# Layer norm statistics on another engine, a later place for a finished half's last pieces in a Mamba scan, and expert products one block ahead

## The chip, the cores and the metric

The kernel runs on one core of a Trainium2 chip. The time is the device time in microseconds of one execution of the whole program, and the time of a kernel is the median over its runs. A core has five engines with a queue of instructions each: TensorE (PE in the profile; its weight loads are shown as PEld), VectorE (DVE), ScalarE (ACT), GpSimd (POOL) and SyncE (SP), which issues DMAs. The engines run beside each other and wait for each other with semaphores; each takes its own instructions in order. What lies in SBUF or in PSUM (TensorE's output memory, 8 banks) has up to 128 partitions, and a tile of "128x512" has 128 partitions of 512 numbers.

## The reference, cut to what matters

The input x has the shape 4 x 1024 x 128: 4 sequences of 1024 tokens, 128 features each, so 4096 tokens. Two blocks are computed one after the other, each with two feed-forward layers around an attention-like layer, with a layer norm ahead of every layer and the layer's result added to x:

```python
x = x + 0.5 * moe(layernorm(x))        # a
x = x + mamba(layernorm(x))
x = x + 0.5 * moe(layernorm(x))        # b, the same weights
x = x + 0.5 * soft(layernorm(x))       # a: soft mixture of experts
x = x + gla(layernorm(x))              # gated linear attention
x = x + 0.5 * soft(layernorm(x))       # b, the same weights

def layernorm(x):                # over the 128 features, no weights
    return (x - mean(x)) / sqrt(var(x) + 1e-5)
```

The three kinds of layer that the change touches, shortened:

```python
def moe(x):       # 8 experts, each token goes to its best 2, limited room
    gates, idx = top_k(softmax(x @ wg), 2); gates /= gates.sum()
    disp = rows of x brought together by expert          # 8 x cap x 128
    h = relu(disp @ w1[e] + b1[e])                       # 512 wide
    out = h @ w2[e] + b2[e]
    return sum over k of gates[k] * valid[k] * out[idx[k], loc[k]]

def mamba(x):     # inner width 256, 16 states
    u, z = split(x @ W_in); u = silu(conv4(u) + conv_b)
    dt, B, C = split(u @ W_xproj); delta = softplus(dt @ W_dt + b_dt)
    h[t] = exp(delta[t] * A) * h[t-1] + delta[t] * B[t] * u[t]   # 256 x 16
    y[t] = sum over states of h[t] * C[t];  y += u * D
    return (y * silu(z)) @ W_out

def gla(x):       # 16 heads of 8
    q, k = silu(x @ Wq), silu(x @ Wk);  v = x @ Wv
    f, g = sigmoid(x @ Wf1 @ Wf2), sigmoid(x @ Wg1 @ Wg2)
    S[t] = f[t] * S[t-1] + k[t] v[t];  o[t] = q[t] . S[t] / sqrt(8)   # S: 8 x 8 per head
    og = o * g;  og = og / sqrt(mean over a head of og^2 + 1e-5)
    return (og * norm_weight) @ Wo
```

The variance of a layer norm is that of the 128 features of one token, mean of squares of the differences from the mean.

## The kernel before

x stays in SBUF as 32 tiles of 128 tokens (NT = 32, each 128 tokens x 128 features), for the whole kernel. Most of the stages are written in a `with tc.manual_schedule(engines=ENGINES)` block, in which the order of the instructions on PE, DVE, ACT and POOL is the order of the Python lines; SP's DMAs are placed by a scheduler. So "ahead of" in the following means ahead in an engine's queue, and an instruction that waits holds up all that stand behind it on its engine.

**Layer norm.** `ln_stats` (L118) takes four tiles: per tile a bn_stats (L121) and a bn_aggr (L122) on DVE give mean and variance, and one add of eps (L123) follows for the four. `ln_root` (L127) takes the power of -1/2 on POOL (L130) and makes -mean * rstd, called nmr, on DVE (L133). `ln_apply` (L141) then normalises a tile in one ACT instruction, with rstd as scale and nmr as bias (L143). The statistics of a layer's norm are taken by the layer before it, when it has added its result to four tiles of x. Behind Mamba and behind gated attention, `ln_root` runs for 16 tiles at a time (around L1560 to L1590), elsewhere for 4.

**Experts** (`moe_layer`, L148). The tokens' normalised rows lie in DRAM; a block of 512 rows of one expert is fetched by four indirect DMAs that POOL issues (`gather`, L346), turned by PE (`turn`, L364, copied by DVE at L366), multiplied by w1 (`hidden`, L374, relu on ACT at L378), multiplied by w2 (`output`, L388) and written back to DRAM by four indirect DMAs of POOL (`scatter`, L352). There are 16 blocks and 64 gathers and 64 scatters per layer. The loop runs, per block, hidden of this block, gathers of the block three ahead (`AHEAD = 3`) between scatters of the block before, turn of the next block, and output of this one. Where no gather is left a `memset` of one column, called spacer, stands in its place (L412). Then the results are read back, weighted (L427 on ACT) and added to x.

**Mamba** (`mamba_layer`, L441). Each sequence is cut into two halves of 512 tokens: 8 halves. A half has 16 steps, one per state n, for all 512 tokens and 256 inner features (NC = 2 groups of 128). Of each state: `fetch` brings B and C to all partitions (DMAs on SP, or for some states a PE product, L610), `feed` makes dBu = du * B (L616 to L620, on POOL for ten states of sixteen, on DVE for six), `decay` makes exp(delta * A) on ACT (L628, twice), `scan` runs the recurrence on DVE (L638, twice), `keep` saves the last state for the next half (L649, ACT), `times_c` multiplies by C on POOL (L654), and `sums` adds up over the states on PE (L663 for the direct term, L669). A half's `prologue` (L484: transposes, convolution, projections, softplus as Ln and Exp at L577, and du and its like on DVE at L579 to L583) is issued in pieces between the steps of the half before it. A half's `epilogue` (L673) is a generator of pieces: zs = zs * py on DVE (L676), the product with W_out on PE (L682), the addition to x on DVE (L688) and the statistics. In the loop over k (state n of half i, k = 16 i + n) the epilogue of a finished half starts at the step with n = 2, and one piece of it is issued per step, ahead of the rest of the step.

**Gated attention** (`gla_layer`, L1318). Also in 8 halves of 512 tokens, with a loop over scan steps k of NU per half; per step PE spreads v over the partitions (L1433), DVE multiplies by k (L1439) and scans (L1450), POOL multiplies by q (L1458), PE sums (L1472). The prologue of the next half (xT copied by ACT at L1402, products on PE at L1407 to L1414, two silus on ACT at L1408, the copy of v at L1412, the thin product at L1416, the gates at L1424) and the epilogue of the one before are issued in pieces between. The epilogue: og on DVE (L1481), its square on ACT (sq, L1485), sums per head on PE (pm, L1489), root and reciprocal (L1494, L1496), spread back (pr, L1499), og again (L1503), the product with Wo on PE (L1506), the addition to x (L1510) and the statistics.

Of the kernel before, what the change touches and what calls it, by code (L numbers as in the profile page):

```python
# [8 lines left out]
F32 = mybir.dt.float32  # L9
# [59 lines left out]
def macaron_kernel(ctx: ExitStack, tc: tile.TileContext, a: dict, out: bass.AP):  # L69
# [67 lines left out]
    def ln_group(ln, j0):  # L137
        ln_stats(ln, j0)
        ln_root(ln, j0)

    def ln_apply(dst, j, ln):  # L141
        _, rstd, nmr = ln
# [5 lines left out]
    def moe_layer(w1, w2, b2, tag, ln, after):  # L148

        xn_d = dram.tile([T, D], F32, name=f"xn_d{tag}")  # L150
        with ExitStack() as s:
# [180 lines left out]


            with ExitStack() as s1:
                gp = s1.enter_context(tc.tile_pool(name=f"gath{tag}", bufs=16))
                wk = s1.enter_context(tc.tile_pool(name=f"ework{tag}", bufs=2))
                yp = s1.enter_context(tc.tile_pool(name=f"ey{tag}", bufs=3))
                ps = s1.enter_context(tc.tile_pool(name=f"eps{tag}", bufs=2, space=PSUM))
                psh = s1.enter_context(tc.tile_pool(name=f"epsh{tag}", bufs=3, space=PSUM))
                NBLK = NSB // 4  # L340
                gs, dTs, hTs, eos = {}, {}, {}, {}
                spacer = wk.tile([P, 1], F32, name="spacer")
# [53 lines left out]

                AHEAD = 3
                with tc.manual_schedule(engines=ENGINES):  # L400
                    for c in range(AHEAD * 4):
                        gather(c)
                    turn(0)
                    for blk in range(NBLK + 1):
                        if blk < NBLK:
                            hidden(blk)
                        for i in range(4):
                            c = (blk + AHEAD) * 4 + i
                            if c < NSB:
                                gather(c)  # L410
                            elif blk > 0:
                                nc.gpsimd.memset(spacer, 0.0)  # L412
                            if blk > 0:
                                scatter((blk - 1) * 4 + i)
                        if blk + 1 < NBLK:
                            turn(blk + 1)
                        if blk < NBLK:
                            output(blk)

# [21 lines left out]
    def mamba_layer(ln, ln_next):  # L441
# [3 lines left out]
        with ExitStack() as s:  # L445
# [227 lines left out]
            def epilogue(r):  # L673

                zs = r["zs"]
                nc.vector.tensor_tensor(zs, zs, r["py"], ALU.mult)  # L676
                yield
                yield
                po = ps.tile([P, NJ, D], F32, name="po", tag="mm")
                for i in range(NJ):  # L680
                    for c in range(NC):
                        nc.tensor.matmul(  # L682
                            po[:, i, :], zs[:, c, i * P : (i + 1) * P], w_out[:, c, :],
                            start=(c == 0), stop=(c == NC - 1),
                        )
                yield
                jj = r["b"] * (S // P) + r["h"] * NJ
                nc.vector.tensor_tensor(  # L688
                    x[:, jj : jj + NJ, :], x[:, jj : jj + NJ, :], po, ALU.add
                )  # L690
                yield
                ln_stats(ln_next, jj, NJ)
                yield


# [8 lines left out]
            with tc.manual_schedule(engines=ENGINES):  # L704

                for _ in prologue(*halves[0], rs[0], psa, "dA"):
                    pass
                for k in range(3):
                    at(fetch, k)
                at(feed, 0)  # L710
                at(feed, 1)
                at(decay, 0)
                at(decay, 1)
                LEAD = 5
                ahead, old, behind = (iter(()) for _ in range(3))
                for k in range(-LEAD, len(units) + 7):
                    if k % DS == DS - LEAD and (k + LEAD) // DS + 1 < len(rs):
                        i = (k + LEAD) // DS + 1
                        old, ahead = ahead, prologue(*halves[i], rs[i])
                    if k < 0:  # L720
                        next(ahead, None)
                        continue
                    if k > DS and k % DS == 2:
                        behind = epilogue(rs[k // DS - 1])
                    next(behind, None)
                    at(fetch, k + 3)
                    at(scan, k)
                    at(keep, k)
                    at(decay, k + 2)
                    at(times_c, k - 1)  # L730
                    at(feed, k + 2)
                    at(sums, k - 2)
                    next(old, None)
                    next(ahead, None)
# [583 lines left out]
    def gla_layer(ln, ln_next):  # L1318
        with ExitStack() as s:
# [158 lines left out]
            def epilogue(u):  # L1478
                r = rs[u]
                og = wk.tile([P, HB], F32, name="og")  # L1480
                nc.vector.scalar_tensor_tensor(  # L1481
                    og, r["po"], HD ** -0.5, r["fg"][:, 1, :], ALU.mult, ALU.mult
                )
                sq = wk.tile([P, HB], F32, name="sq")
                nc.scalar.activation(sq, og, AF.Square)  # L1485

                pm = ps.tile([P, P], F32, name="pm", tag="mm")
                for i in range(4):
                    nc.tensor.matmul(  # L1489
                        pm[i * 32 : (i + 1) * 32, :], hsel, sq[:, i * P : (i + 1) * P],  # L1490
                        start=True, stop=True,
                    )
                rn = wk.tile([P, P], F32, name="rn")
                nc.scalar.activation(rn, pm, AF.Sqrt, bias=eps_t, scale=1.0 / HD)  # L1494
                yield
                nc.vector.reciprocal(rn, rn)  # L1496
                pr = ps.tile([P, HB], F32, name="pr", tag="mm")
                for i in range(4):
                    nc.tensor.matmul(  # L1499
                        pr[:, i * P : (i + 1) * P], hback[:, i, :], rn, start=True, stop=True  # L1500
                    )
                yield
                nc.vector.scalar_tensor_tensor(og, og, nw, pr, ALU.mult, ALU.mult)  # L1503
                py = ps.tile([P, NJ, D], F32, name="py", tag="mm")
                for i in range(NJ):
                    nc.tensor.matmul(  # L1506
                        py[:, i, :], og[:, i * P : (i + 1) * P], wo, start=True, stop=True
                    )
                yield
                nc.vector.tensor_tensor(  # L1510
                    x[:, u * NJ : (u + 1) * NJ, :], x[:, u * NJ : (u + 1) * NJ, :], py, ALU.add
                )
                ln_stats(ln_next, u * NJ)
                yield


# [46 lines left out]
    spool2 = ctx.enter_context(tc.tile_pool(name="softw2", bufs=1, side="right"))  # L1563
    ew, eb = expert_weights(spool2)
    for j in range(0, NT, 16):
        ln_root(lns[2], j, 16)
    moe("b", lns[2], lambda j: ln_group(lns[3], j))

    def rest(soft):
        soft("a", lns[3], lambda j: ln_group(lns[4], j))  # L1570
        gla_layer(lns[4], lns[5])
        for j in range(0, NT, 16):
            ln_root(lns[5], j, 16)
        soft("b", lns[5], last=True)

    bounded = nc.values_load(flag, min_val=0, max_val=1)
# [87 lines left out]
```

## Time and profile before

| quantity | value |
|---|---|
| median of 9 runs | 2324.6 us |
| lowest and highest of them | 2322.81 and 2333.39 us |
| profiled execution, its own time | 2333.12 us |
| its span, first to last instruction | 2331.3 us |
| mean granted clock of TensorE in it | 0.911 |
| PE busy | 1926.1 us (83%) |
| DVE busy | 1412.7 us (61%) |
| POOL busy | 1397.4 us (60%) |
| ACT busy | 929.1 us (40%) |

By stage, from the timeline of the profiled execution: experts a with their routing to about 276 us, Mamba 276 to 860, experts b to about 1140, soft a 1140 to 1640, gated attention 1640 to 1830, soft b 1830 to 2331. The granted clock is the share of full speed at which TensorE was let run.

How to read the profile's lines. In the list of groups a line has the source line, engine, operation, output and inputs, their shapes and the count; then busy us in all and mean ns of one; then the engine's idle time just before these instructions, and what ended most of it ("<-DVE hst L638" is: DVE's work on hst at line 638). In the timeline a line has start, duration (of the whole run of like instructions, "x6" being six), engine, source line, operation, tiles, and in brackets the idle time before and its releaser. "issue" is time in which an engine waited for nothing that the profile shows.

### The profile page before, as it was taken

To read this page: it belongs to the slowest core of one execution; us is meant where nothing else is said; L and a number is where in the kernel's file an instruction comes from. 1 tells how busy PE (TensorE), PEld (TensorE's weight loads), DVE (VectorE), ACT (ScalarE), POOL (GpSimd) and SP (SyncE) were. 2 spreads that over 40 slices of the span, in tenths; PEclk is the share of its full clock that TensorE was granted. 3 is DMA by queue.
4 is the path that set the end of the run, shared out by engine and by line. 5 is a ranking of instruction groups with operands and counts; after the bars stand their busy time and mean duration, and the time that the engine had idled before them with its cause. 6 is when DMAs were issued, how large, how long until landed. Compare 5 with 4: busy or idle time off the path is not lost. (4 is left out here: it accounts for less than half of the span.)

```text
span 2331.3 us, 17972 instructions
## 1 busy us (share of the span) xinstructions
PE 1926.1 (83%) x5889; PEld 902.5 (39%) x5889; DVE 1412.7 (61%) x1947; ACT 929.1 (40%) x1453; POOL 1397.4 (60%) x896
## 2 busy tenths in 40 slices
PE   4788267889888855875499989999889799989998
PEld 3565122333333224654144434444223344434443
DVE  4311548898888965111777764556787677754444
ACT  3232265666555523322333333332553333333331
POOL 2677248888888961776355556664444455556663
PEclk9999679989999985898699999999897799999999
DMA  6111332323223233112100000000000000000000
GB/s 244 37 51 51 97 114 92 114 92 115 96 92 113 102 134 94 51 53 78 38 0 1 1 1 1 1 0 0 6 1 0 1 0 0 1 1 5 10 10 15
DMA packets 63677, 111.23 MB, mean 48 GB/s; under 512 B 7999, under 2 KB 41423, under 8 KB 58581
## 3 DMA queue, kind: packets, MB, share of 16 engines
q1 hardware_dynamic: 45062, 81.37, 10.5%
q0 software_dynamic: 8192, 16.79, 2.3%
q10 hardware_dynamic: 10322, 11.85, 1.5%
q8 instruction: 48, 0.79, 0.1%
q14 instruction: 53, 0.43, 0.1%
HBM read 90.53 MB, written 19.44 MB: 47 GB/s over the span
## 5 line engine op out<-in xcount | busy, mean ns | idle before, releaser
L891 POOL TENSOR_TENSOR dm<-ex,sm 128x1024 f32<-128x1024 f32 x128 | 244.6, 1911 | 218.2 <-DVE sm L887 125.3
L654 POOL TENSOR_TENSOR hc<-hst,Cs 128x1024 f32<-128x1024 f32 x128 | 287.9, 2260 | 78.2 <-DVE hst L638 74.8
L669 PE MATMUL py<-hc,ident 128*128 128x512 f32 x512 | 280.3, 679 | 44.2 <-POOL hc L654 44.0
L999 POOL TENSOR_TENSOR acc<-acc,L 128x1024 f32<-128x1024 f32 x96 | 225.9, 2353 | 117.1 <-ACT L L991 116.4
L991 ACT ACTIVATE L<-pl,pbc 128x512 f32<-128x512 f32 x256 | 162.1, 684 | 284.3 <-PE pl L981 279.9
L870 PE MATMUL l<-phiT,xT 128*128 128x512 f32 x512 | 245.8, 604 | 15.4 <-ACT xT L861 8.7
L879 ACT ACTIVATE ex<-l,nmh 128x1024 f32<-128x1024 f32 x128 | 142.7, 1115 | 285.2 <-DVE nmh L874 283.1
L981 PE MATMUL pl<-xT,phiM 128*128 128x512 f32 x512 | 245.2, 604 | 0.0
L1025 PE MATMUL py<-L,yt 128*128 128x512 f32 x512 | 238.4, 593 | 4.4 <-DVE L L1015 4.4
L902 PE MATMUL px<-dm,xn 128*128 128x512 f32 x512 | 240.8, 593 | 0.9 <-POOL dm L891 0.9
L874 DVE TENSOR_REDUCE nmh<-l 128x1 f32<-128x1024 f32 x128 | 156.6, 1223 | 107.5 <-PE l L870 107.5
L628 ACT ACTIVATE dA<-delta,A 128x512 f32<-128x512 f32 x256 | 179.3, 722 | 94.2 <-DVE hst L638 91.3
L620 POOL TENSOR_TENSOR dBu<-du,Bs 128x1024 f32<-128x1024 f32 x80 | 172.8, 2160 | 39.5 <-ACT dA L628 39.5
L669 PEld LDWEIGHTS py<-hc,ident 128*128 128x128 f32 x512 | 98.2, 206 | 209.1 <-issue 122.4
L378 ACT ACTIVATE hT<-ph,cols 128x512 f32<-128x512 f32 x128 | 88.0, 687 | 219.6 <-PE ph L374 216.4
L638 DVE TENSOR_TENSOR_SCAN hst<-dA,carry,dBu 128x512 f32<-128x512 f32 x128 | 154.2, 1260 | 5.6 <-POOL dBu L620 5.6
L886 DVE TENSOR_REDUCE sm<-ex 128x32 f32<-128x1024 f32 x128 | 154.8, 1209 | 0.0
L870 PEld LDWEIGHTS l<-phiT,xT 128*128 128x128 f32 x512 | 97.1, 193 | 145.8 <-issue 115.1
L638 DVE TENSOR_TENSOR_SCAN hst<-dA,dBu 128x512 f32<-128x512 f32 x128 | 146.6, 1200 | 7.6 <-POOL dBu L620 7.5
L352 POOL DMA_INDIRECT y_d<-eo,dest x128 | 125.9, 983 | 35.7 <-issue 24.1
L1015 DVE TENSOR_TENSOR L<-L,rd 128x1024 f32<-128x1024 f32 x128 | 147.0, 1212 | 0.1
L1025 PEld LDWEIGHTS py<-L,yt 128*128 128x128 f32 x512 | 96.8, 190 | 127.3 <-issue 117.0
(248 smaller groups left out, 2897.3 us busy)
## 6 DMA issues: line engine op xcount, KB each, us to landing
Cs<-bc_d SPq DMA_DIRECT2D x32, 1024.0 KB, 4.6
Bs<-bc_d SPq DMA_DIRECT2D x80, 256.0 KB, 3.1
w<-in_w SPq DMA_DIRECT2D x4, 2048.0 KB
y<-y_d SPq DMA_DIRECT2D x32, 256.0 KB, 3.5
y_d<-zero SPq DMA_DIRECT2D x1, 4096.0 KB
ew<-in_ew ACTq DMA_DIRECT2D x1, 4096.0 KB
x<-in_x SPq DMA_DIRECT2D x8, 256.0 KB, 7.9
xn_da<-xn ACTq DMA_DIRECT2D x8, 256.0 KB, 14.4
```

The source lines that it names most:

```text
L620: eng.tensor_tensor(dBu, r["du"], r.pop(("B", n)).unsqueeze(2).to_broadcast([P, HB, NC]), ALU.mult,)
L628: nc.scalar.activation(dA, r["delta"][:, :, c], AF.Exp, scale=A[:, c * DS + n : c * DS + n + 1],)
L638: nc.vector.tensor_tensor_scan(hst[:, :, c], r.pop(("dA", n, c)), dBu[:, :, c], 0.0 if h == 0 else carry[b][:, c, n : n + 1], ALU.mult, AL ...
L654: nc.gpsimd.tensor_tensor(hc, r.pop(("h", n)), Cs.unsqueeze(2).to_broadcast([P, HB, NC]), ALU.mult)
L669: nc.tensor.matmul(r["py"][:, c, :], ident, hc[:, :, c], start=False, stop=(n == DS - 1))
L870: nc.tensor.matmul(l[:, q * 512 : (q + 1) * 512], xT[:, j * P : (j + 1) * P], phiN[:, o : o + 512], start=True, stop=True,)
L891: nc.gpsimd.tensor_tensor(dms[k], exs.pop(k), sms.pop(k).unsqueeze(2).to_broadcast([P, NG, PS]), ALU.mult,)
L902: nc.tensor.matmul(px[hf * 2 + q], xns[j // 4][:, j % 4, :], dmf[:, q * 512 : (q + 1) * 512], start=(j == 0), stop=(j == NT - 1),)
L981: nc.tensor.matmul(pl[:, i, :], phiM[:, (2 * c + i) * P : (2 * c + i + 1) * P], xT[:, t * TB : (t + 1) * TB], start=True, stop=True,)
L991: nc.scalar.activation(L[:, i, :], pl[:, i, :], AF.Exp, bias=pbc[:, 2 * c + i : 2 * c + i + 1], scale=-1.0,)
L999: nc.gpsimd.tensor_tensor(accs[t], accs[t], L, ALU.add)
L1025: nc.tensor.matmul(pys[t], yt[:, 2 * c + i, :], L[:, i, :], start=(c + i == 0), stop=(c == CS - 1 and i == 1),)
```

## The change: two sets of statistics on ScalarE, a reordered step, one more block in flight

There are three parts.

1. In the experts' loop the transposes run two blocks ahead and the first product one block ahead of the second; gathers are issued four blocks ahead. Buffers grow with it: 20 gathered tiles instead of 16, 3 work buffers instead of 2, 4 PSUM buffers of the first product instead of 3.
2. In Mamba's loop the piece of a finished half's epilogue is issued after `fetch` and `scan` of the step and no longer ahead of them.
3. The statistics behind Mamba and behind gated attention are taken by a new function on ACT: four Copies with their sums accumulated, one small instruction that makes -mean, four Squares of x - mean with their sums accumulated, one small instruction that makes var + eps. They use the same three tiles per layer norm. The root follows in a new function with both its instructions on POOL.

```diff
+    def ln_stats_act(ln, j0, n=4):
+        mv, rstd, nmr = ln
+        js = slice(j0, j0 + n)
+        junk = small.tile([P, D], F32, name="junk")
+        for j in range(j0, j0 + n):
+            nc.scalar.activation(junk, x[:, j, :], AF.Copy, accum_out=mv[:, j, 0:1])
+        nc.scalar.activation(nmr[:, js], mv[:, js, 0], AF.Copy, scale=-1.0 / D)
+        for j in range(j0, j0 + n):
+            nc.scalar.activation(
+                junk, x[:, j, :], AF.Square, bias=nmr[:, j : j + 1], accum_out=mv[:, j, 1:2]
+            )
+        nc.scalar.activation(
+            rstd[:, js], mv[:, js, 1], AF.Identity, bias=eps_t, scale=1.0 / D
+        )
+
+    def ln_root_pool(ln, j0, n=4):
+        _, rstd, nmr = ln
+        js = slice(j0, j0 + n)
+        nc.gpsimd.tensor_tensor(
+            rstd[:, js], rstd[:, js], half_t.to_broadcast([P, n]), ALU.pow
+        )
+        nc.gpsimd.tensor_tensor(nmr[:, js], nmr[:, js], rstd[:, js], ALU.mult)
...
-                gp = s1.enter_context(tc.tile_pool(name=f"gath{tag}", bufs=16))
-                wk = s1.enter_context(tc.tile_pool(name=f"ework{tag}", bufs=2))
+                gp = s1.enter_context(tc.tile_pool(name=f"gath{tag}", bufs=20))
+                wk = s1.enter_context(tc.tile_pool(name=f"ework{tag}", bufs=3))
...
-                psh = s1.enter_context(tc.tile_pool(name=f"epsh{tag}", bufs=3, space=PSUM))
+                psh = s1.enter_context(tc.tile_pool(name=f"epsh{tag}", bufs=4, space=PSUM))
...
-                AHEAD = 3
+                AHEAD = 4
                 with tc.manual_schedule(engines=ENGINES):
                     for c in range(AHEAD * 4):
                         gather(c)
                     turn(0)
+                    turn(1)
+                    hidden(0)
                     for blk in range(NBLK + 1):
-                        if blk < NBLK:
-                            hidden(blk)
+                        if blk + 2 < NBLK:
+                            turn(blk + 2)
+                        if blk + 1 < NBLK:
+                            hidden(blk + 1)
                         for i in range(4):
...
-                        if blk + 1 < NBLK:
-                            turn(blk + 1)
                         if blk < NBLK:
                             output(blk)
...
-                ln_stats(ln_next, jj, NJ)
+                ln_stats_act(ln_next, jj, NJ)
...
-                    next(behind, None)
                     at(fetch, k + 3)
                     at(scan, k)
+                    next(behind, None)
                     at(keep, k)
...
-                ln_stats(ln_next, u * NJ)
+                ln_stats_act(ln_next, u * NJ)
...
     for j in range(0, NT, 16):
-        ln_root(lns[2], j, 16)
+        ln_root_pool(lns[2], j, 16)
...
         for j in range(0, NT, 16):
-            ln_root(lns[5], j, 16)
+            ln_root_pool(lns[5], j, 16)
```

## The prediction

> **What bounds the kernel now.** I read first the shares, then the costliest groups by shape, then the timeline of each stage that the diff touches, because no engine bounds the whole span. TensorE (PE) is busy 83% of it, but the two soft stages (1140 to 1640 and 1830 to 2331 us), where it is the bound, are not touched. Of the touched rows the groups say:
>
> ```profile
> L654 POOL TENSOR_TENSOR hc<-hst,Cs 128x1024 f32<-128x1024 f32 x128 | 287.9, 2260 | 78.2 <-DVE hst L638 74.8
> L352 POOL DMA_INDIRECT y_d<-eo,dest x128 | 125.9, 983 | 35.7 <-issue 24.1 <-DMA y_d<-eo,dest 6.1 <-DVE dT L366 5.2
> L121 DVE BATCH_NORM_STATS2 st<-x 128x6 f32<-128x128 f32 x192 | 51.8, 280 | 7.9 <-DMA x<-in_x 7.4
> L143 ACT ACTIVATE xn<-x,nmr,rstd 128x128 f32<-128x128 f32 x192 | 83.2, 483 | 25.0 <-issue 15.4 <-DVE nmr L133 7.4 <-DMA xn_da<-xn 2.2
> L427 ACT ACTIVATE y<-y,gate 128x128 f32<-128x128 f32 x64 | 20.3, 389 | 42.5 <-DMA y<-y_d 26.6 <-DVE y L431 11.8 <-DVE x L435 2.8
> L676 DVE TENSOR_TENSOR zs<-zs,py 128x1024 f32<-128x1024 f32 x8 | 9.8, 1221 | 40.8 <-PE py L669 40.8
> L649 ACT COPY carry<-hst 128x2 f32<-128x2 f32 x64 | 12.2, 190 | 88.1 <-DVE hst L638 87.6
> ```
>
> In **Mamba** (276 to 860 us, halves about 67.6 us apart by the starts of zs, 399.27 and 466.89) POOL, DVE and PE are nearly level at 57 to 59 us of work per half, so a wait passes from one to the next. At a half's end zs holds up DVE, and all scans behind it, until the last sum is done. Here it is, DVE and then POOL:
>
> ```profile
> 399.27 1.22 DVE L676 TENSOR_TENSOR zs<-zs,py 128x1024 f32<-128x1024 f32 x1 [4.91 <-PE py L669]
> 400.41 7.15 DVE L638 TENSOR_TENSOR_SCAN hst<-dA,carry,dBu 128x512 f32<-128x512 f32 x6
> ```
> ```profile
> 403.03 2.14 POOL L654 TENSOR_TENSOR hc<-hst,Cs 128x1024 f32<-128x1024 f32 x1 [3.00 <-DVE hst L638]
> ...
> 418.19 2.13 POOL L654 TENSOR_TENSOR hc<-hst,Cs 128x1024 f32<-128x1024 f32 x1 [2.56 <-DVE hst L638]
> ```
>
> The first POOL wait (3.00) comes from zs, the second (2.56) from the statistics, which held DVE from 413.16 to 415.66 ahead of two scans.
>
> In the **experts** POOL's indirect DMAs are the bound: one every 1.28 us from 75.4 to 239.2 us (0.97 to 0.99 busy, 0.30 between), 128 of them, with no larger hole, while PE waits for each block's gathers:
>
> ```profile
> 208.43 0.33 PE L364 MATMUL pt<-ident,g 128*128 128x128 f32 x1 [2.28 <-DMA g<-xn_da,src]
> ```
>
> In **gated attention** (1640 to 1830) the clock of PE decides, as the table by windows shows; its columns are busy time of PE, weight loads, DVE, ACT, POOL, then the granted clock:
>
> ```profile
> 1680.00:1700.00 20.00, 17.37 (x78) 5.77 (x76) 18.88 (x27) 10.91 (x18) 9.72 (x5) 1.00 0.00 0
> 1740.00:1760.00 20.00, 18.64 (x59) 6.58 (x56) 14.80 (x22) 6.92 (x13) 9.45 (x4) 0.74 0.00 1
> ```
>
> At full clock DVE sets a half's time (18.88 of 20): 19.4 us from og to og. From 1720 on, a half takes 23.8 us, and the bound is a loop: sq on ACT, PE's output products, xT, PE's next projections, the v copy, sq. In it ACT waits for PE, and PE for ACT:
>
> ```profile
> 1715.14 0.59 ACT L1412 COPY qkv<-pq 128x512 f32<-128x512 f32 x1 [1.74 <-PE pq L1411]
> 1716.12 0.58 ACT L1416 COPY lr<-p 40x512 f32<-40x512 f32 x1 [0.40 <-PE p L1414]
> ```
> ```profile
> 1738.41 0.43 PE L1489 MATMUL pm<-sq,hsel 128*32 128x128 f32 x8 [1.27 <-ACT sq L1485]
> ```
>
> **The new statistics, S per four tiles.** Off DVE go 4 bn_stats, 4 bn_aggr and the add: 2.4 us in place. On ACT come 10 instructions, each behind the one before; no row of the trace has an accumulating one. From below: four Copies with a scale as the L427 row (0.389) and four Squares with a bias the same, plus two of 0.19 (the smallest row, L649): 3.5. From above: eight of 0.483 (L143, two pointers) and an extra 0.19 each for reading the accumulator out, and the two small ones: 5.8. A Square resembles L143 less than L427, but every sum must leave the engine, so I take 0.389 + 0.19 for each of eight, and 0.38: S = 5.0. Copy, Square and Identity bring no table load: the compiled kernels have 85 each.
>
> The Trainium skill, "ScalarE: Activation LUTs", Rules for kernel authors, says that such elementwise work belongs on VectorE and not on ScalarE. The rows agree as far as they go (2.4 us against 3.5 to 5.8), and by the rule alone both moves would lose; whether they do is decided by which engine has slack.
>
> **Mamba.** Two things leave DVE's path. fetch and scan now stand ahead of zs, so one scan (2.4 us) runs in the 4.91 us wait; fetch has PE's pb product or SP's Bs and Cs reads in it, and these only come sooner; the epilogue issues no DMA. zs stays where it was, since PE ends the last sum at 399.24. Retimed by hand, the product of state 2 starts 3.0 us sooner; that of state 6 is then held by PE's sums (three hc buffers, the third sum ends at 414.9), so 3.1 of the 5.56 is left. Against it: on ACT the statistics stand behind the silu block (408.34 to 411.6) and two decays, ahead of the decay of state 8, the copy of dbc and the next half's softplus. With S = 5.0 the scan of state 8 gains 2.2 us at most; the softplus, for which DVE then waits (three waits on ACT l, 29.3 us, of which one at the stage's start is 28.2), 1.2 to 2.5. I take 2.0 for each of six boundaries, and the whole 2.6 for the seventh, where the statistics are the only stall (822.57): 6 x 2.0 + 2.6 = **-14.6**. Bounds: all zs and statistics stalls at the seven (42.6 in sum) gone from below; 1.0 a boundary, -8, from above. The cover is ACT's 44 us of work in 67.6; without it S stands on the path, +2.6 a half.
>
> **Roots on POOL.** nmr moves behind pow for four 128x16 groups: it saves a 0.475 row of DVE and adds at most the pow's 2.9 on POOL. One of the two in gated attention stands amid waits of 1.3 to 5.1 us there; the others lie in the tails, and are in what follows.
>
> **Experts.** The 128 DMAs on POOL and their order by kind stay, four spacers of 0.12 come in, so 164 us stay. Twenty gathers instead of sixteen go ahead of the first scatter, at 101.7, when PE's first block ends at 101 to 102: 0 to 0.8 late. At the end POOL has five blocks of pure scatters (5.1 us each from 213.3), PE takes 8.4 us a block, and block 14 is ready at 228.6 as its slot comes: 0 to 3 late. I take **+1.3** for both layers (0 to +4); nothing can be gained while POOL's pitch holds.
>
> **Gated attention.** The 2.4 us leave DVE, which is the bound only at full clock. On ACT they stand between silu and the v copy, whose waits (1.74 and 0.40) swallow a part; sq comes 5.0 - 2.14 = 2.9 later once, and then each half's loop is longer. At a clock as in 1740 to 1760: 23.9 + 2.9 = 26.8. At full clock the loop is ACT's 10.4, S, and waits of 0.42, 4.39 and about 0.6: 20.8, against 19.4. Behind sq, PE's pm waits, with the spread and sums of the next states behind it, and DVE's scans behind those. PE's gap there grows from 1.3 to between 2.6 and 3.5 us.
>
> What that does to the clock is the largest unknown. Gaps of 1.27 to 1.40 us in this stage were followed by half clock in four of six halves; gaps of 2.5 to 3 in Mamba (423 to 426, 446 to 453) were; those of 2.2 in the experts (granted 0.97 there) mostly not. I take the first half at full clock, as its gap of 1.4 was harmless before, and the rest at half: intervals 19.5, 20.9, 23.9, 23.8 become 20.8, 26.8, 26.8, 26.8, which is +1.3 +5.9 +2.9 +3.0, with the first delay 2.9: **+16.0**. All at full clock: 2.9 + 1.3 - 0.1 - 3.1 - 3.0 = -2.0. All at half: +22.0.
>
> The page "TensorE: Matmul & The Clock Gate" of the Trainium skill (Part 1) has the clock halve only after an idle window of about 3.4 us. The 1.27 us gap above, with half clock from 1740.7, speaks against that being all; by the page the stage would mostly keep its clock, an estimate of -2 for the loop.
>
> Later than the loop: the last two halves have no projections, ACT has 10 to 17 us free before sq, but sq of the last stands behind the statistics of the one before, and soft b's first xT copy behind three of the last four Squares: **+2.5** (2 to 3).
>
> **Sum.** -14.6 + 1.3 + 16.0 + 2.5 = +5.2. The profiled execution took 2333.1 (span 2331.3 and 1.8 around), 8.5 above the median of nine, 2324.6; the difference is put on the median: 2338.3 on the profile's scale, **2329.8** on the median's.
>
> **Rivals.**
> *Clock kept (faster).* PE never loses its clock in gated attention, since the new gap (2.6 at full clock) is nearer to the experts' harmless 2.2. The point from which it decides: at most one of the four intervals at half clock. Loop -2.0, Mamba at 2.2 a boundary -15.8, others +3.8: -14.0, 2310.6. Against it: 1.3 us sufficed before.
> *ACT is next late in Mamba.* The statistics hold back the decays; 1.0 a boundary and 2.6: -8.6, and +11.2 in all, 2335.8. For it: DVE already waits on ACT for l. Against: ACT's 88.1 us of idle time at L649.
> *Half clock in every half of gated attention.* +22.0 in place of +16.0: 2335.8.
> *The experts turn PE-bound at their ends:* +4 in place of +1.3, 2332.5.
> *POOL's stalls in Mamba vanish as a whole,* -30 with some PE pitch left: +16.0 + 2.5 + 1.3 - 30 = -10, 2314.4. Against: hc buffers wait for PE's sums.
>
> **How the numbers follow.** Forecast 0.30 (own range 2325 to 2336), clock kept 0.25, ACT late 0.20, every half 0.14, experts 0.04, stalls gone 0.07. The measurement can tell about 0.2%, 4.65 us. Faster: 0.25 + 0.07 + 0.04 of the forecast = 0.36. Same: 0.12 of the forecast and 0.03 of ACT late = 0.15. Slower: 0.14 + 0.17 + 0.14 + 0.04 = 0.49. Range: low by clock kept and Mamba's 17, others +2: 2324.6 - 17 = 2308; high by 22.0 + 3 + 4 - 8 = +21: 2346.
>
> **What would show it.** Mamba: a scan within zs's wait, POOL's 3.00 and 2.56 replaced by one wait of about 2.5 on PE or less, halves of 65.5. Statistics: ten rows on ACT, 5 us per group. Experts: 1.28 us pitch kept, at the end a POOL wait on eo under 2 us. Gated attention: sq to sq of 26.8, a PE wait of over 2.5 before pm, clock below 0.8 in most windows from 1700 on. The prediction is wrong if that stage keeps clock 1.00, if S is outside 3.5 to 5.8, or if Mamba's halves shorten by under 1 or over 4 us.

## The result and the profile after

The changed kernel takes 2341.9 us (median of 10 runs, 2339.95 to 2343.81), the kernel before 2327.22 (median of all its 31 runs up to then). The ratio is 1.0058, with a 95% interval of 1.0046 to 1.0071: slower by 13.5 us, 10.7 to 16.5. (A ratio is taken over all runs; it can differ by up to 0.12% from that of the two medians, which are 14.7 us apart here.) The forecast was +5.2, in the range and on the right side, but too small.

The profiled execution of the changed kernel took 2341.14 (span 2339.1), so it lies at its median; that of the kernel before was 5.9 above its own. So the two spans differ by 7.8 us only, and the table shares out these 7.8. Each stretch runs from one landmark of the timeline to another; for og and sq that is the start of the instruction:

| stretch (from the starts and ends in the timelines) | before | after | difference |
|---|---|---|---|
| experts a, first gather to last scatter | 163.8 | 164.4 | +0.6 |
| Mamba, first scan to last | 530.4 | 510.2 | -20.2 |
| experts b, first gather to last scatter | 163.3 | 163.2 | -0.1 |
| soft a, first product, to the first og of gated attention | 537.3 | 534.4 | -2.9 |
| gated attention, first og to last sq | 145.1 | 179.6 | +34.5 |
| last sq to soft b's first product | 12.6 | 12.8 | +0.2 |
| soft b, first product to the issue of the last DMA | 492.2 | 491.6 | -0.6 |

So a gain of 20 in Mamba was paid back 1.7 times in gated attention. The stretches that are not in the table (start, routing, reading back, end) make -3.7 together.

The groups of the changed kernel by shape, which answer to those shown of before; columns as there. Source lines are 25 to 27 higher here: L681 is the product that was L654, L377 the scatter that was L352, L168 the old L143, L454 the old L427, L703 zs, L676 the carry that was L649.

```profile
L681 POOL TENSOR_TENSOR hc<-hst,Cs 128x1024 f32<-128x1024 f32 x128 | 290.6, 2279 | 57.1 <-DVE hst L665 32.1 <-PE py L696 21.9 <-issue 2.0
...
L377 POOL DMA_INDIRECT y_d<-eo,dest x128 | 125.8, 982 | 35.6 <-issue 24.5 <-DVE dT L391 4.9 <-DMA y_d<-eo,dest 4.9
...
L121 DVE BATCH_NORM_STATS2 st<-x 128x6 f32<-128x128 f32 x128 | 32.6, 270 | 6.9 <-DMA x<-in_x 6.6
...
L150 ACT ACTIVATE junk<-x,nmr 128x128 f32<-128x128 f32 x64 | 25.6, 401 | 1.9
...
L147 ACT ACTIVATE junk<-x 128x128 f32<-128x128 f32 x64 | 19.8, 309 | 42.7 <-DVE x L1537 25.5 <-DVE x L715 15.5
...
L147 ACT ACTIVATION_READ_ACCUMULATOR junk<-x 128x1 f32 x64 | 12.1, 189 | 0.0
...
L676 ACT COPY carry<-hst 128x2 f32<-128x2 f32 x64 | 12.0, 187 | 65.3 <-DVE hst L665 65.0
L150 ACT ACTIVATION_READ_ACCUMULATOR junk<-x,nmr 128x1 f32 x64 | 11.9, 187 | 0.0
...
L703 DVE TENSOR_TENSOR zs<-zs,py 128x1024 f32<-128x1024 f32 x8 | 9.7, 1217 | 26.9 <-PE py L696 26.9
```

POOL's wait for the scans at L681 fell from 74.8 to 32.1 us, and 21.9 us of waiting for PE's sums took part of its place. zs waits 26.9 in place of 40.8. The 64 Copies and 64 Squares are new, and behind each stands an instruction of its own that reads the accumulator out. Per group of four tiles: 4 x (0.309 + 0.189) + 4 x (0.401 + 0.187), and 0.204 and 0.296 for the small ones, 4.84 us. They overlap a little: in the half shown below, the first starts at 1699.09 and the copy of v behind the last at 1703.38, so they hold ACT's queue for 4.29 us.

Mamba, the same half's end as shown of before. DVE:

```profile
393.21 2.45 DVE L665 TENSOR_TENSOR_SCAN hst<-dA,carry,dBu 128x512 f32<-128x512 f32 x2
399.29 1.22 DVE L703 TENSOR_TENSOR zs<-zs,py 128x1024 f32<-128x1024 f32 x1 [3.63 <-PE py L696]
...
418.04 4.81 DVE L665 TENSOR_TENSOR_SCAN hst<-dA,carry,dBu 128x512 f32<-128x512 f32 x4 [1.43 <-ACT dA L655]
```

And POOL:

```profile
399.39 2.13 POOL L681 TENSOR_TENSOR hc<-hst,Cs 128x1024 f32<-128x1024 f32 x1 [1.02 <-issue]
401.48 2.14 POOL L647 TENSOR_TENSOR dBu<-du,Bs 128x1024 f32<-128x1024 f32 x1
404.49 2.13 POOL L681 TENSOR_TENSOR hc<-hst,Cs 128x1024 f32<-128x1024 f32 x1 [0.87 <-PE py L696]
408.39 2.15 POOL L681 TENSOR_TENSOR hc<-hst,Cs 128x1024 f32<-128x1024 f32 x1 [1.78 <-PE py L696]
...
415.02 2.13 POOL L681 TENSOR_TENSOR hc<-hst,Cs 128x1024 f32<-128x1024 f32 x1 [0.29 <-PE py L696]
```

One scan runs ahead of zs, whose own start has not moved (399.27 before, 399.29 now). The product that was held up by 3.00 us starts at 399.39 in place of 403.03, and from then on PE's sums release POOL. The later one that stood behind the statistics starts at 415.02 in place of 418.19. State 8's scan starts at 418.04, and now waits for ACT. Before, it was the second of the three pairs of scans in this line, and started at 421.42:

```profile
419.05 7.15 DVE L638 TENSOR_TENSOR_SCAN hst<-dA,carry,dBu 128x512 f32<-128x512 f32 x6
```

Gated attention, ACT's queue in one half:

```profile
1703.17 0.30 ACT L153 ACTIVATE rstd<-mv,eps_t 128x4 f32<-128x4 f32 x1
1703.38 0.56 ACT L1439 COPY qkv<-pq 128x512 f32<-128x512 f32 x1
1703.84 0.58 ACT L1443 COPY lr<-p 40x512 f32<-40x512 f32 x1
1704.32 0.63 ACT L1512 ACTIVATE sq<-og 128x512 f32<-128x512 f32 x1
...
1727.88 1.28 ACT L1435 ACT_TABLE_LOAD   x1 [8.08 <-PE pq L1434]
```

And PE in the same half, with the windows of the stage behind it (columns as before; the clock is the number ahead of the last two):

```profile
1705.00 0.65 PE L1516 MATMUL pm<-sq,hsel 128*32 128x128 f32 x8 [3.01 <-ACT sq L1512]
1705.58 2.08 PE L1460 MATMUL pv<-qkv,spread_w 32*128 32x512 f32 x4
...
1728.73 1.13 PE L1460 MATMUL pv<-qkv,spread_w 32*128 32x512 f32 x4
```
```profile
1640.00:1660.00 20.00, 16.90 (x68) 4.92 (x66) 18.76 (x17) 12.87 (x22) 10.10 (x6) 1.00 0.00 0
...
1680.00:1700.00 20.00, 18.65 (x51) 7.40 (x50) 11.86 (x11) 6.29 (x15) 7.04 (x3) 0.57 0.00 0
1700.00:1720.00 20.00, 15.64 (x45) 5.06 (x45) 11.29 (x12) 10.85 (x27) 4.69 (x2) 0.60 0.00 0
1720.00:1740.00 20.00, 16.83 (x48) 5.29 (x48) 9.74 (x11) 10.75 (x27) 7.04 (x3) 0.67 0.00 1
```

PE waits 3.01 us for sq, and behind that the same four spreads take 2.08 us in place of 1.13: the granted clock is 0.50 from 1704.1 to 1728.0. ACT, whose queue is 4.29 us longer, then idles 8.08 us for PE's products, where before it idled 4.39:

```profile
1711.01 1.28 ACT L1408 ACT_TABLE_LOAD   x1 [4.39 <-PE pq L1407]
```

From sq to sq the halves take 21.2, 31.1, 31.1, 31.0, 25.6, 24.2 and 14.8 us, where before they took 19.3, 19.5, 20.9, 23.9, 23.8, 24.3 and 12.7.

### The profile page after: what moved, and what is told of

Same layout as the page of the kernel before. It is cut to its first block, busy times and chain, and to the rows that moved or that the text cites. A ratio compares the mean times of both kernels' runs of the same rounds, so it can differ in the third digit from the quotient of the medians.

```text
span 2339.1 us, 18123 instructions
## 1 busy us (share of the span) xinstructions
PE 1936.4 (83%) x5889; PEld 905.3 (39%) x5889; DVE 1378.6 (59%) x1799; ACT 986.2 (42%) x1741; POOL 1398.9 (60%) x908
## 3 DMA queue, kind: packets, MB, share of 16 engines
q1 hardware_dynamic: 45062, 81.37, 10.2%
## 4 chain that ended last, share of the span: by engine, by line
PE 55%; DVE 12%; ACT 9%; POOL 5%; DMA 5%; issue 4%; ACTq 0%; SPq 0%; POOLq 0%; DVEq 0%
PE l L897 9%; PE pl L1008 9%; PE py L1052 8%; PE px L929 8%; PE py L696 3%; PE pu L548 3%; DMA g<-xn_db,src 3%; DVE hst L665 2%; PE pv L1460 2%; ACT dA L655 2%; PE po L1499 1%; DMA w<-in_w 1%; PE ph L399 1%; POOL y_d L377 1%; ACT junk L150 1%
## 5 line engine op out<-in xcount | busy, mean ns | idle before, releaser
L681 POOL TENSOR_TENSOR hc<-hst,Cs 128x1024 f32<-128x1024 f32 x128 | 290.6, 2279 | 57.1 <-DVE hst L665 32.1
L696 PE MATMUL py<-hc,ident 128*128 128x512 f32 x512 | 274.3, 666 | 44.2 <-POOL hc L681 44.0
L897 PE MATMUL l<-phiT,xT 128*128 128x512 f32 x512 | 245.4, 604 | 15.7 <-ACT xT L888 9.1
L665 DVE TENSOR_TENSOR_SCAN hst<-dA,dBu 128x512 f32<-128x512 f32 x128 | 147.3, 1203 | 16.5 <-POOL dBu L647 10.6
L1485 POOL TENSOR_TENSOR qs<-st,qkv 128x1024 f32<-128x1024 f32 x32 | 75.2, 2349 | 124.8 <-DVE st L1477 119.5
L377 POOL DMA_INDIRECT y_d<-eo,dest x128 | 125.8, 982 | 35.6 <-issue 24.5
## 6 DMA issues: line engine op xcount, KB each, us to landing
xn_da<-xn ACTq DMA_DIRECT2D x8, 256.0 KB, 14.8
```

The source lines that it names most:

```text
L665: nc.vector.tensor_tensor_scan(hst[:, :, c], r.pop(("dA", n, c)), dBu[:, :, c], 0.0 if h == 0 else carry[b][:, c, n : n + 1], ALU.mult, AL ...
L681: nc.gpsimd.tensor_tensor(hc, r.pop(("h", n)), Cs.unsqueeze(2).to_broadcast([P, HB, NC]), ALU.mult)
L696: nc.tensor.matmul(r["py"][:, c, :], ident, hc[:, :, c], start=False, stop=(n == DS - 1))
L897: nc.tensor.matmul(l[:, q * 512 : (q + 1) * 512], xT[:, j * P : (j + 1) * P], phiN[:, o : o + 512], start=True, stop=True,)
```

## The experiments

A ratio is always to the kernel before on the same chip. e1 to e4 ran on one chip, e5 to e8 and e12 on a second, e9 to e11 on a third, on which the kernel before took 2388.05 us in place of 2328.47 to 2329.94; so only ratios and stage times are compared across.

### Which part does what

e1, with gated attention's statistics back on DVE:

```diff
-                ln_stats_act(ln_next, u * NJ)
+                ln_stats(ln_next, u * NJ)
...
-            ln_root_pool(lns[5], j, 16)
+            ln_root(lns[5], j, 16)
```

> The changed kernel with gated attention's statistics back on DVE (and their root's second step on DVE), all else as changed. Theory A (gated attention alone loses, Mamba gains): from the first og of that stage to its last sq the changed profile took 179.6 us against 145.1 before, and it stood 25.9 us ahead at the stage's start; so this kernel is faster than before by 15 to 26 us, about 2305 beside 2327, and its stage takes 143 to 149 us again. Rival B (the clock in that stage differs from one execution to the next, and the statistics have little to do with it): the stage stays above 160 us, and the kernel is within 10 us of before.

Measured: 2307.81 beside 2329.66, ratio 0.9911 (0.9893 to 0.9929); first og to last sq 140.5 us. Theory A: the loss goes with this one part.

e2, the kernel before with that part alone (the two lines of e1 the other way round, and the new functions):

> The kernel before with only gated attention's statistics moved to ACT. Theory A: slower than before by 28 to 36 us (the stage's first og to last sq about 175 to 180 us, 31 us from sq to sq where PE is at half clock), granted clock below 0.7 in most windows of the stage. Rival B: slower by under 15 us, sq to sq below 27 us as the prediction had it. Rival C (the loss needs Mamba's or the experts' parts too): no change.

Measured: 2360.7, ratio 1.0137 (1.0119 to 1.0156), +31.0 between the medians; the stretch 175.0 us; halves 21.2, 31.1, 31.1, 25.6, 27.1, 22.6, 15.7. Theory A: the loss needs nothing else. The product of the two ratios, 0.9911 x 1.0137 = 1.0047, agrees with the whole change (1.0046 to 1.0071).

e4, the experts' part alone (the hunks of the diff in `moe_layer` put into the kernel before):

> The kernel before with only the experts' part of the change. If POOL's pitch of 1.28 us per indirect DMA is the bound, first gather to last scatter stays at 163 to 165 us in both layers and the time within 3 us of before (+1.3 by the prediction). If deeper prefetch helped after all, 3 us or more faster; if PE became the bound at the ends, 3 to 8 us slower, with a POOL wait on eo of over 2 us there.

Measured: 2329.54, ratio 0.9996 (0.9983 to 1.0008); first gather to last scatter 164.9 and 163.7 us. No change on that chip.

e8, Mamba's order alone:

```diff
-                    next(behind, None)
                     at(fetch, k + 3)
                     at(scan, k)
+                    next(behind, None)
```

> The kernel before with only Mamba's epilogue pieces moved behind fetch and scan, the statistics still on DVE. The whole Mamba part is worth 21 us (first to last scan 530.4 us before, 508 to 510 with both). If the scan in the wait of zs is the main part, this gives 10 to 14 us; if the statistics on DVE are, 6 to 9; if the two only work together, under 4.

Measured: 2308.45, ratio 0.9923 (0.9903 to 0.9943), -17.9 (-13.3 to -22.6); first scan to last 508.2 us, no longer than with both parts (508.2 in e1, 510.2 in the changed kernel; with Mamba as before, e2 has 527.2 and e4 528.5). That is above what was expected of it: the whole of Mamba's gain. POOL in e8:

```profile
397.58 2.13 POOL L654 TENSOR_TENSOR hc<-hst,Cs 128x1024 f32<-128x1024 f32 x1 [1.02 <-issue]
399.67 2.14 POOL L620 TENSOR_TENSOR dBu<-du,Bs 128x1024 f32<-128x1024 f32 x1
402.67 2.12 POOL L654 TENSOR_TENSOR hc<-hst,Cs 128x1024 f32<-128x1024 f32 x1 [0.86 <-PE py L669]
...
413.20 2.13 POOL L654 TENSOR_TENSOR hc<-hst,Cs 128x1024 f32<-128x1024 f32 x1 [0.30 <-DVE rstd L123]
```

The statistics are still on DVE here, and yet the wait that they caused is down from 2.56 to 0.30: DVE got ahead by one scan, and POOL is paced by PE's sums in between.

e9, Mamba's statistics alone:

```diff
-                ln_stats(ln_next, jj, NJ)
+                ln_stats_act(ln_next, jj, NJ)
...
-        ln_root(lns[2], j, 16)
+        ln_root_pool(lns[2], j, 16)
```

> The kernel before with only Mamba's statistics moved to ACT, its order unchanged. The order alone left POOL's second wait at 0.30 us in place of 2.56, so there the move had nothing left to win. If the two parts compete for the same slack (theory P: PE's sums set the pace once zs no longer holds up DVE): alone the move still takes away the 2.56 of each of seven boundaries, 8 to 15 us faster, although it adds nothing to the order. If POOL's first wait (3.00, from zs) is then simply longer or ACT is late with the decay of state 8 (theory L): within 4 us of before.

Measured: 2377.89 beside 2388.05, ratio 0.9966 (0.9953 to 0.9978), -8.1 (-5.3 to -11.2): the lower end of theory P. Part of theory L is seen too: the wait behind the statistics is gone, the one behind zs is longer, at this half's end 4.69 us in place of 3.00:

```profile
432.67 2.14 POOL L679 TENSOR_TENSOR hc<-hst,Cs 128x1024 f32<-128x1024 f32 x1 [4.69 <-DVE hst L663]
```

### What makes gated attention lose

e3, the changed kernel with products on PE ahead of pm whose output is overwritten later; they do nothing but keep PE busy:

```diff
+                if u + 1 < len(halves):
+                    for _ in range(2):
+                        nc.tensor.matmul(
+                            rs[u + 1]["po"][64:, :], hback[:, 0, :64],
+                            hback.rearrange("p i q -> p (i q)"), start=True, stop=True,
+                        )
                 pm = ps.tile([P, P], F32, name="pm", tag="mm")
```

> The changed kernel, and ahead of pm in gated attention two 64x512 products into rows of a PSUM tile that are overwritten later, so PE does not stand idle while ACT takes the statistics. Theory A1 (the larger part of the loss is the clock, lost because PE stands idle 3 us ahead of pm): clock of 0.95 or more in most windows, sq to sq 20 to 22 us in place of 31, the stage 130 to 140 us, faster than the changed kernel by 35 to 45 us and than before by 20 to 30. Theory A2 (the chain through ACT alone): the extra products leave the clock below 0.75 and sq to sq at 29 to 32; the time stays within 5 us of the changed kernel.

Measured: 2323.24, ratio 0.9967 (0.9954 to 0.9980); the stretch 157.6 us, in place of 179.6. Halves of 21.2, 21.2, 27.0, 22.8, 27.2, 24.1: in between. 2.1 to 2.2 us of idle time stayed ahead of pm.

e5, six such products:

> As e3_fill_pe_gap, with six products in place of two. There two took 0.9 us of the 3.0 and left a gap of 2.1; halves whose clock stayed full took 21.2 us from sq to sq, the others 23 to 28. Theory A1 (half clock follows the idle time ahead of pm): six cover it (6 x 0.48 = 2.9), the clock is 0.95 or more in all windows from 1660 to 1780, sq to sq 21 to 22 throughout, 12 to 22 us faster than e3, about 2303 to 2311. Theory A2 (the gap is not what the clock follows): sq to sq stays at 23 to 28 in half of the halves, the time within 5 us of e3's 2323.

Measured: 2320.98, ratio 0.9968 (0.9955 to 0.9982), the stretch 156.2. A miss: a product is two passes of PE and takes 0.88 us, not 0.48, so six outlast the gap and hold up pm themselves: it starts 1.8 us behind sq (1680.88, 1682.70), where 0.7 is usual. Its time doesn't tell the theories apart. But PE never waits ahead of pm here until the last half, and the granted clock still falls to 0.50 three times in the five halves from the first sq to the sixth, for 6.8, 3.4 and 6.8 us: half clock doesn't need this wait.

e12, three:

> As e3 and e5, with three products: six in e5 took 5.3 us where 3.0 were idle and so stood on the path themselves (halves of 22.3 to 25.4); a product takes 0.88 us, three 2.6. Theory A1 (the clock follows the idle time ahead of pm): nothing is added to the path and at most 0.5 to 1.2 us stays idle, so every half takes 20.9 to 21.5 us at clock 0.95 or more, first og to last sq 140 to 146, 24 to 32 us faster than the changed kernel, 0.985 to 0.992 of before. If other waits of PE (at fg 0.7 us, at xT 0.7 us) are enough for the clock to fall: some windows at 0.6 to 0.85 and halves of 21 to 26, first og to last sq 148 to 156.

Measured: 2304.73, ratio 0.9893 (0.9870 to 0.9916), the stretch 140.3 us, halves of 21.3, 22.7, 21.2, 21.2, 22.8, 17.6. The windows:

```profile
1660.00:1680.00 20.00, 17.44 (x72) 5.85 (x74) 15.44 (x16) 13.83 (x34) 8.14 (x5) 0.98 0.00 1
1680.00:1700.00 20.00, 17.28 (x67) 5.21 (x63) 14.46 (x15) 12.09 (x30) 9.24 (x4) 0.94 0.00 1
1700.00:1720.00 20.00, 17.96 (x78) 6.12 (x78) 15.93 (x16) 13.20 (x33) 9.44 (x4) 1.00 0.00 1
1720.00:1740.00 20.00, 17.29 (x76) 5.92 (x74) 15.87 (x16) 12.98 (x34) 10.42 (x6) 1.00 0.00 0
```

Theory A1, though two halves still lost the clock for 3.4 us each. The gap is not gone, since the first products ran beside the one ahead of them (see e10); what stays of 3.0 to 3.3 us is 1.34 to 1.37 in these halves:

```profile
1673.03 0.42 PE L1522 MATMUL pm<-sq,hsel 128*32 128x128 f32 x8 [1.36 <-ACT sq L1512]
```

Nothing was taken off ACT and 2.6 us of useless work per half was put on PE, and the stage is 39 us shorter than in the changed kernel. With the clock kept, the statistics on ACT cost the chain 21.2 - 19.4 = 1.8 us a half.

e6, the statistics a half later, where ACT waits for PE anyway:

```diff
@@ epilogue(u), behind the products py
+                if u > 0:
+                    ln_stats_act(ln_next, (u - 1) * NJ)
                 yield
...
-                ln_stats_act(ln_next, u * NJ)
+                if u == len(halves) - 1:
+                    ln_stats_act(ln_next, u * NJ)
```

> The changed kernel, with a half's statistics in gated attention issued on ACT three steps later, behind the next half's copy of xT, where ACT idles 4.4 to 8.1 us for PE's products, and no longer between silu and the copy of v. Theory A (the place in ACT's queue costs, not ACT's 4.9 us): sq no longer waits for them, the gap ahead of pm falls to 1.3 or less, sq to sq 17 to 22 us, first og to last sq at or below the 140 to 145 us of before; 30 to 40 us faster than the changed kernel, 2302 to 2312. Theory D (ACT's added work itself is the cost): sq to sq stays above 26 and the time within 8 us of the changed kernel's 2342.

Measured: 2301.53, ratio 0.9887 (0.9869 to 0.9905); the stretch 134.5 us, 10.6 less than in the profile of before, and less than in any other run with the stage as before (140.5 in e1, 140.7 in e9, 143.4 in e4, 145.0 in e8). Halves of 19.3, 19.3, 20.8, 20.9, 23.7, 19.9 and 10.0. At the end of the second one, which kept full clock:

```profile
1692.30 0.42 PE L1516 MATMUL pm<-sq,hsel 128*32 128x128 f32 x8 [1.20 <-ACT sq L1512]
```

PE waits 1.20 us for sq, and the silu begins 4.98 us behind the copy of xT, at 1686.04 after 1681.06, where before it was 4.97 (1711.01 after 1706.04). Theory A: the same work on ACT costs nothing there.

e7, e1 with three filling products:

> e1_gla_stats_on_dve with three such products ahead of pm, which cover the 1.3 us that PE waits there with the statistics on DVE. Theory A1: the half clock of that stage goes, every half takes 19.3 to 20 us in place of 19.4 to 24, 10 to 16 us faster than e1 (2292 to 2298). Theory A2: within 4 us of e1's 2308.

Measured: 2301.56, ratio 0.9883 (0.9863 to 0.9902), the stretch 135.9 us beside 140.5 of e1. About 6 us by the ratios, whose intervals overlap: less than theory A1 expected, more than A2. PE no longer waits ahead of pm in the first seven halves, and yet the clock fell in three of the first six (23.0, 21.5 and 22.0 us).

e10, e6 with one such product, and e11, e6 with Mamba's statistics on DVE:

> e6_stats_a_half_later with one product (0.9 us) in the 1.2 us that PE still waits ahead of pm. If the clock follows idle time there: four halves of 19.3 to 20 us where e6 has 20.8 to 23.7, 4 to 9 us faster than e6, 2292 to 2298. If other waits of PE (0.68 twice per half) keep the clock falling: within 3 us of e6's 2301.5.

> e6_stats_a_half_later with Mamba's statistics back on DVE. By theory P (the order alone brings Mamba's gain) within 3 us of e6, 2299 to 2305. If the move of Mamba's statistics has a part of its own: 5 us or more slower than e6.

Measured: 2352.85 and 2350.82 beside 2388.05, both 0.9856 (0.9839 to 0.9874 and 0.9835 to 0.9876). The times can't be held against the expected ones, as the chip is another; the stretches can: 135.7 and 137.5 us beside 134.5 in e6. e10 is a miss: halves of 25.1 and 22.4 are still there, as in e11. It tells nothing of the clock, because the single product ran at the same time as the thin product p ahead of it and left the wait at 1.17 us, where e11 has 1.20:

```profile
1739.67 0.62 PE L1441 MATMUL p<-xT,wfg 128*40 128x512 f32 x1
1739.68 0.64 PE L1516 MATMUL po<-hback 128*64 128x512 f32 x1
1740.13 0.59 PE L1441 MATMUL p<-xT,wfg 128*40 128x512 f32 x1
1740.16 0.59 PE L1516 MATMUL po<-hback 128*64 128x512 f32 x1
1741.92 0.43 PE L1522 MATMUL pm<-sq,hsel 128*32 128x128 f32 x8 [1.17 <-ACT sq L1512]
```

e11 fits theory P by its Mamba, 510.6 us from first to last scan beside 508.1 in e10; a difference of 2.5 us is as large as that between like kernels (508.2 in e12, 510.2 in the changed one).

The runs side by side, over the five halves from the first sq to the sixth. Half clock is the time at a granted clock of 0.50; the waits are those ahead of pm behind the first five sq:

| kernel | waits of PE ahead of pm, us | five halves, us | of them at half clock, us |
|---|---|---|---|
| before | 1.27 to 1.56 | 107.4 | 23.9 |
| changed | 1.57, then 3.0 to 3.3 | 139.9 | 81.9 |
| e2 | 1.56, then 3.0 to 3.2 | 136.0 | 71.7 |
| e3 | 0.68, then 2.1 to 2.2 | 119.3 | 30.7 |
| e12 | none, then 1.36 to 1.37 | 109.0 | 6.8 |
| e6 | 1.57, then 1.20 | 103.9 | 17.1 |
| e7 | none | 103.2 | 10.2 |
| e5 | none, but pm is held up | 120.9 | 17.1 |

So waits of 3 us go with far more half clock than all others, and filling them takes it away: that is the loss. Below that the wait ahead of pm does not decide alone: before and e12 wait about as long and differ by 17 us, and e5 and e7 lose the clock without it.

## Why the prediction was right in direction and too small

**Experts: right.** +1.3 was forecast for both layers; +0.6 and -0.1 in the profile, no change of the time in e4. The pitch of 1.28 us is the bound there, and no wait on eo appeared at the end.

**S: right.** 5.0 us forecast, 4.84 measured as a sum and 4.29 in ACT's queue, between 3.5 and 5.8. The accumulator's read-out, taken from the 0.19 of the smallest row, is 0.188; as that row is a copy of 128x2, the close fit is luck. The Copies (0.309) came out shorter than the 0.389 taken for them, the Squares (0.401) a little longer. No table load was added: both profiles have 57.

**Mamba: the mechanism right, the size too small, and the credit wrong.** -14.6 was forecast, -20.2 in the profile, -17.9 for the order alone. The step that failed is "I take 2.0 for each of six boundaries". From zs to zs, three of the six came out 3.2 us shorter (67.62 to 64.43, twice, and 67.61 to 64.37), which is the 3.1 of the retiming by hand, one 5.4, and two about 1; the seventh, forecast at 2.6, gave 4.4. By the prediction's own sign ("under 1 or over 4 us") two of the six, 0.9 and 5.4, lie outside, though their mean of 2.8 does not. The limit of 2.2 through ACT was drawn with the silu block left where it was (from 408.34), but the decays ahead of it came sooner with the earlier scan, and the block began at 407.11: 1.2 us, so state 8's scan gained 3.4. And the statistics, of which the prediction had a whole stall to win, contribute nothing once the order is changed (e8, e1, e11); alone they are worth 8.1 (e9). The two parts win the same slack: with the order changed, it is PE's sums that POOL waits for next (0.87 and 1.78 us above).

**Gated attention: the mechanism right, the price about half of the real one.** +16.0 and +2.5 were forecast, +34.5 is in the profile and +31.0 in e2. PE's wait ahead of pm came as forecast (2.6 to 3.5 us; measured 3.0 to 3.3), and at full clock the loop did too: 20.8, measured 21.2 in the two inner halves of e12 that kept it. Two terms were mis-sized. "I take the first half at full clock" gave 20.8 to a half that took 31.1: 10.3 of the missing 16 us. "At a clock as in 1740 to 1760: 23.9 + 2.9 = 26.8" was then the price of three more halves, of which two took 31.1 and 31.0 (8.5 us more) and the last 25.6. Its fault is the window taken: in the half around it PE ran at half clock for 10.2 of 23.9 us (0.74 in the window), and the new delay was added to that as if the clock stayed. In the changed kernel half clock lasts from 1704.1 to 1728.0, 23.9 of 31.1 us (0.57 to 0.67 in the windows), and as long in the halves on either side, so that most of a half's products take nearly twice the time. Over the five halves half clock grew by 58.0 us; at half speed that is 29 us of work lost, an estimate, of the 32.5 by which they grew. e12 shows that this is the price: with 1.4 us of the wait left, the clock is 0.94 to 1.00 and 39 us are gone. Why half clock lasts 10 us in one case and 24 in another stays open; the wait does not decide it alone, as in the changed kernel the longest of the four (3.32 us, ahead of the half of 25.6) was followed by the shortest fall, 10.2.

**Inside the range with some luck.** Mamba gained 5.6 us more than forecast and gated attention lost 16.0 more. With Mamba as forecast the kernel would have stood at about 2347, an estimate, just above the range's upper end of 2346.

**The roots on POOL** were not tried by themselves; what they do lies in the stretches that moved by under 1 us. **The rivals:** "clock kept" fell; "half clock in every half" came nearest, with the price of a half wrong; "ACT is next late in Mamba" fell, though the wait on ACT that it named is there (1.43 us ahead of state 8's scan). The experts' +4 did not come, nor did -30 in Mamba.

**Better than both:** e6 (0.9887), e7 (0.9883), e12 (0.9893), and on the third chip e10 and e11 (0.9856). e8, which only moves one line, has 0.9923.

## What to carry to other kernels

Before work is moved to an idle engine, look at what stands behind it in that engine's queue: 4.8 us of statistics cost 31 us ahead of an instruction that TensorE waits for, and nothing a few steps later, where the engine waited anyway. A longer wait of TensorE can put most of the products behind it at half clock, so its upper price is that, and not a mean clock from the profile; filling the gap with useless products is a quick test, once the trace shows that they do fill it. Two edits that free the same engine at the same point may win the same slack, so cost the second with the first in place.

## What the runs showed of the hardware

- An activation with an accumulated sum is two instructions: a 128x128 Copy of 0.309 us and a read-out of 0.189; a Square with a bias pointer 0.401 and 0.187. Four of each with two small ones sum to 4.84 us and hold the queue for 4.29.
- Half clock on TensorE can last far longer than the wait ahead of it: waits of 3.10, 3.01 and 3.17 us ahead of pm were followed by 23.9 us at half clock each, one of 3.32 by 10.2; waits of 1.20 us in e6 by none once and by 3.4, 3.4 and 10.2 in the halves behind. The Trainium skill, "TensorE: Matmul & The Clock Gate", Part 1, ties the fall to an idle window of about 3.4 us and the return to a busy one of the same length. Here the clock falls in e7 at 1682.6 though no wait of PE in the 20 us before is over 0.68 us, and PE's run without a wait from 1712.20 to 1719.18 in the changed kernel, twice 3.4 us long, did not bring it back. The length of the falls does agree with a step of that size: 3.4, 6.8, 10.2 and 23.9 us are 1, 2, 3 and 7 times 3.41.
- Two narrow products can run on TensorE side by side: in e10 one with weights of 128x40 and one of 128x64 start at 1739.67 and 1739.68 and last 0.62 and 0.64 us.
- The third chip was 2.5% slower with the same kernel, and its experts took far longer: first gather to last scatter 195.4 and 193.3 us in e9 with the old loop, 188.7 to 189.3 in e10 and e11 with the new one, where the other two chips have 163 to 165 with either. There the block ahead was worth 4 to 7 us a layer, which fits the lower ratios of e10 and e11. On it POOL waits for eo, which DVE copies out behind the second product: 34.3 us in e9's first experts layer and 24.8 in e10's. What holds up the products there stays open.
